# Layer 1's queries and keys projected densely and moved into padded strips by DMA, the first group's squares on ScalarE, and groups of 3, 4, 5 and 4 sequences

## The chip, the cores and the metric

The kernel runs on one core of one Trainium2 chip. The metric is the device time of one execution in microseconds (us). The kernel before took 1684.3 us, the median of three runs (1683.4, 1684.3, 1684.37).

## What is computed

Sixteen sequences of 512 tokens with 128 features pass through two transformer layers, all in float32. With LN for the normalization of a token's features without weights:

```
n  = LN(x)
x1 = x + linear_attention(n) + mixture_of_experts(n)          # layer 0
n1 = LN(x1)
y  = x1 + softmax_attention(n1) + channel_mix(n1)             # layer 1
```

Both attentions have 16 heads of 8 features. The linear attention of layer 0 uses rotated queries and keys and a running sum. The mixture has 8 experts with 512 hidden features (`square(relu(h @ w_fc)) @ w_proj`); a router picks two for every token and weighs them, and a shared expert of the same form works on all tokens. Layer 1's attention lets the queries of a chunk of 64 tokens see all keys up to the end of their chunk; its probabilities are scaled by a factor that is computed from their row sum, then normalized again. The channel mix blends each token with the one before it, and computes `sigmoid(r) * (square(relu(k)) @ W_v)`.

Layer 1's score needs q and k alone:

```
qkv    = n1 @ W_qkv.T                     # (16, 512, 384), in heads of 8
scores = einsum('bhtd,bhsd->bhts', q_c, k_c) * 8 ** -0.5
```

## The kernel before

**An order that is planned.** The program isn't emitted as it is written. A recording layer (class `Program`, from line 225) takes every operation with the tiles that it reads and writes (`call`, line 247; `add`, line 289), and `run` (line 330) then emits them by a list schedule: each engine takes, of the operations whose inputs its cost table says are ready, the one that comes first in the recorded order. The costs stand in lines 213 to 216: a DMA on SP's queue has 80 ns of issue and, besides, a landing time from its bytes (line 273); a weight load of two DMAs has 300 ns. The resulting order on each engine is fixed in the program. SyncE (SP) issues all plain DMAs in this one order, so that a DMA whose wait isn't over holds up those behind it; GpSimd does the same with its squares and its indirect DMAs. Every operation is emitted by one helper, so that the profile gives line 259 for nearly all of them; the names of their tiles tell them apart.

**Groups.** Tokens are sent to their experts in groups of sequences, `GROUPS = (3, 4, 4, 3, 2)` (line 47). For each group, `dispatch` (line 1038) normalizes the sequences, routes their tokens, and writes them sorted by expert into rows in DRAM (an indirect DMA for each 128 tokens and each of the two experts, line 1091). Each expert's rows are padded to whole tiles of 128; a group of n sequences has `(2 * 4n * 128 + 8 * 127) // 128` slot tiles (`slot_count`, line 53): 23, 31, 39 and 47 for n = 2, 3, 4 and 5. `slot_tiles` (line 1122) runs over them four at a time: fetch rows `xg`, transpose them, load each tile's expert weights `wf` and `wp` (256 KB each, four buffers of each; lines 1146 and 1149), multiply, relu on ScalarE, square, multiply, and write `results` to DRAM. The square of a first pair runs on GpSimd, that of a second pair on VectorE, and in group 0 all on VectorE (line 1177).

**Layers.** `layer0` runs the linear attention and the shared expert of a group's sequences one by one; their x1 goes to DRAM. `layer1` takes the sequences of the group before. Its sequences overlap: `body(b)` (line 1529) weighs the values of sequence b, and in between its steps are those of `operands(b, 1)` and then of `head(b + 1)` (line 1510), which ends with `operands(b + 1, 0)`. `head` gathers the experts' results from DRAM (`combine`, line 1215: two times four indirect DMAs into a tile `back` with two buffers, each added to x1), normalizes, transposes into `xp`, and does the channel mix and the values.

**Operands of layer 1's attention** (`operands`, line 1294). A score matmul has 32 rows, four side by side in TensorE. The 16 heads are worked in pairs, eight heads as a half u (0 or 1), so that a half has four strips of 32 rows. A strip holds a pair's 16 features and, behind them, rows with constants: they hide the keys that a query may not see, and take the row maximum of each head. So that q and k land in strips, the projection's weights are padded: `wqk1` has 4 blocks of 128 columns, of which 64 are used. Each half takes two 128x512 matmuls (tile `qk`). VectorE adds constants on the way from PSUM: `qa` is the query part plus `aug_q`; `ka` has two versions, one for each head of the pair, each the key part times a 0/1 column (`parity`) plus `aug_k`. Then the scores (`sc`) are computed once for their row maxima (VectorE, tile `maxima`), the maxima are transposed (`mx`) and subtracted in `qa`, and `weighted` (line 1349) computes the transposed scores (`st`), their exponentials on ScalarE (`ex`) and the product with the values (`o`). `qa` and `ka` have two buffers each.

The functions that the change touches:

Of the kernel before, what the change touches and what calls it, by code (L numbers as in the profile page):

```python
# [45 lines left out]

GROUPS = (3, 4, 4, 3, 2)
FIRST = [sum(GROUPS[:g]) for g in range(len(GROUPS))]
# [4 lines left out]
def slot_count(gt):  # L53
# [31 lines left out]
    ("causal", P), ("rank", E), ("upper", P), ("ones", P), ("tile", SLOT_TILES),  # L85
    ("aug_q", T), ("aug_k", 2 * T), ("parity", 2),
)
# [70 lines left out]
class Base:  # L158


    def __init__(self, slots, make):
        self.slots, self.make, self.tile = slots, make, None
        self.writers, self.readers = [], []
        self.left, self.free_at, self.users = 0, 0.0, []
# [60 lines left out]
class Program:  # L225
# [21 lines left out]
    def call(self, name, api, method, args, kw):  # L247
        views = [a for a in (*args, *kw.values()) if isinstance(a, View)]
        o = kw.get("out", args[0] if args else None)
        writes = [o.base] if isinstance(o, View) else []  # L250
        reads = [v.base for v in views if v is not o]
        n = math.prod(o.shape[1:]) if isinstance(o, View) else 0
        later = 0.0

        def made(a):
            return a.made() if isinstance(a, View) else a

        def emit():
            return getattr(api, method)(*map(made, args), **{k: made(a) for k, a in kw.items()})  # L259

        if name == "PE":
            later = 60.0
            form = (args[1].shape[0], o.shape[0])
            if method == "transpose":
                cost = 112.0
            elif args[1].shape[0] == 32:
                cost = max(0.425 * n, 56.0)
            elif o.shape[0] == 32:
                cost = max(0.425 * n, 56.0)
            else:  # L270
                cost = max(1.68 * n, 224.0)
        elif method == "dma_start":
            cost, later = 80.0, 512.0 * n
        else:
            form = method if (name, method) in COSTS else None
            if name == "DVE" and method in ("tensor_scalar", "tensor_scalar_min", "tensor_scalar_max"):
                form = "fast"
            if method in ("tensor_reduce", "bn_stats"):
                n = math.prod(args[1].shape[1:])
            least, each = COSTS[name, form]  # L280
            cost = least + each * n
            if kw.get("func", args[2] if len(args) > 2 else None) == AF.Sqrt:
                cost += 2600.0
        op = self.add(name, emit, reads, writes, cost, later)
        if name == "PE":
            (self.unit_of[0] if self.unit_of else op).form = form
        return op

    def add(self, name, emit, reads, writes, cost, later=0.0):
# [11 lines left out]
        for base in writes:  # L301

            op.needs.update(o for o in base.writers if o.engine != "SP" or name != "SP")
            op.needs.update(base.readers)
        for base in reads:
            base.readers.append(op)
        for base in writes:
            if base.readers:
                base.writers, base.readers = [], []
            base.writers.append(op)  # L310
# [176 lines left out]
def two_layers(ctx: ExitStack, tc: tile.TileContext, x, small, const, w_fc, w_proj, out):  # L487
# [32 lines left out]

    const_sb = fixed.tile([P, _CONST_N], F32, tag="const", name="const_sb")
    small_sb = fixed.tile([P, _STAYS_N], F32, tag="small", name="small_sb")
# [14 lines left out]
    x_in = {b: load_x(b, "x_in", 2) for b in range(2)}  # L537
    lo = _CONST_AT["aug_q"][0]
    SP.dma_start(const_sb[:, 0:lo], const[:, 0:lo])
    raw = {}  # L540
# [5 lines left out]
    for names in (_STAYS[:2], _STAYS[2:]):  # L546
# [3 lines left out]
        SP.dma_start(small_sb[:, slo:shi], small[:, lo:hi])  # L550
    lo = _CONST_AT["aug_q"][0]
    SP.dma_start(const_sb[:, lo:], const[:, lo:])
    program.lag = 250
# [25 lines left out]
    sin = c_("sin").rearrange("p (t d) -> p t d", d=4)  # L579
    aug_k = c_("aug_k").rearrange("p (o t) -> p o t", o=2)  # L580

    program.lag = 200

    wqk1 = fixed.tile([P, 4, 4, 32], F32, tag="wqk1", name="wqk1")
    G.memset(wqk1, 0.0)
    given1 = raw["wqk1"].rearrange("p (su j o e) -> p su j o e", su=4, j=4, o=2)
    for o in range(2):
        V.tensor_copy(wqk1[:, :, :, o * DH : (o + 1) * DH], given1[:, :, :, o, 0:DH])

# [532 lines left out]
    def slot_tiles(g):  # L1122
# [41 lines left out]
        def hidden(xgT, ws, q, pair):  # L1164
# [11 lines left out]

            (V if pair or g == 0 else G).tensor_tensor(o, o, o, ALU.mult)
            return h
# [36 lines left out]
    def combine(x1, b):  # L1215
# [4 lines left out]
        for j in range(2):  # L1220
            y = p2.tile([P, NT, D], F32, tag="back", name=f"back_{b}_{j}", bufs=2)
            for t in range(NT):
# [70 lines left out]

    def operands(xT, b, u):

        ps = big(f"qk1_{b}_{u}")
        for i in range(2):
            M.matmul(
                ps[:, i, :], wqk1[:, 2 * i + u, :, :].rearrange("p j e -> p (j e)"), xT,
                start=True, stop=True,
            )
        qa = p2.tile([P, T], F32, tag="qa", name=f"qa_{b}_{u}")
        V.tensor_tensor(qa, ps[:, 0, :], c_("aug_q"), ALU.add)
        ka = p2.tile([P, 2, T], F32, tag="ka", name=f"ka_{b}_{u}")
        for o in range(2):  # L1310
            V.scalar_tensor_tensor(
                ka[:, o, :], ps[:, 1, :], c_("parity")[:, o : o + 1], aug_k[:, o, :],
                ALU.mult, ALU.add,
            )
        yield
# [25 lines left out]
        for t in range(NT):  # L1341
            M.transpose(
                pm[:, t * P : (t + 1) * P], mx[:, t, :, :].rearrange("p j e -> p (j e)"), ident
            )
        V.tensor_tensor(qa, qa, pm, ALU.subtract)
        yield
        return qa, ka

# [161 lines left out]
    def head(b):  # L1510
# [6 lines left out]
        yield from combine(x1, b)  # L1517
        xp = p2.tile([P, T + 1], F32, tag="xp", name=f"xp_{b}", bufs=2)
        G.memset(xp[:, 0:1], 0.0)
        yield from layernorm_T(x1, xp[:, 1 : T + 1], f"1_{b}", "xn1", 1)  # L1520
        yield
        base = yield from channel_mix(x1, xp, b)
        yield
        vp = values(xp[:, 1 : T + 1], b)
        yield
        qm, ka = yield from operands(xp[:, 1 : T + 1], b, 0)
        return xp, base, vp, qm, ka

    def body(b, state):


        xp, base, vp, qm, ka = state
        o0, (qm, ka) = yield from weighted(
            qm, ka, vp, b, 0, operands(xp[:, 1 : T + 1], b, 1), 2
        )
        o1, got = yield from weighted(qm, ka, vp, b, 1, head(b + 1), 3)
        behind1.append(tail([o0, o1], base, b))
        return got
# [61 lines left out]
def _constants():  # L1600
# [14 lines left out]
    aug_q, aug_k = np.zeros((4, 32, T), f), np.zeros((4, 32, 2, T), f)  # L1615
    parity = np.zeros((4, 32, 2), f)
    for o in range(2):
        aug_k[:, PAIR + o, o] = 1.0
        parity[:, o * DH : (o + 1) * DH, o] = 1.0
    for t in range(NT):  # L1620
        aug_q[:, PAIR + 2 + t, t * P : t * P + P // 2] = HIDDEN
        aug_k[:, PAIR + 2 + t, :, t * P + P // 2 : (t + 1) * P] = 1.0
    c["aug_q"], c["aug_k"] = aug_q.reshape(P, T), aug_k.reshape(P, 2 * T)
    c["parity"] = parity.reshape(P, 2)
    inv = (f(10000.0) ** (-np.arange(4, dtype=f) / f(4))).astype(f)
# [65 lines left out]
```

## Time and profile before

| | |
|---|---|
| median of the runs | 1684.3 us |
| profiled execution, its own time | 1683.1 us |
| its span in the trace | 1681.3 us |
| TensorE matmul (PE) busy | 1566.0 us, 93% |
| VectorE (DVE) busy | 1220.5 us, 73% |
| ScalarE (ACT) busy | 763.4 us, 45% |
| GpSimd (POOL) busy | 405.0 us, 24% |
| mean granted TensorE clock | 0.973 |
| mean transfer | 100 GB/s |

All durations below come from the one profiled execution. A group's row reads: line, engine, operation, output and input tiles with their shapes, count; then busy time in us and mean ns of one; then the idle time of the engine just before them, and what ended it. PEld is the weight load that overlaps the matmuls. A float32 matmul has two records in the trace, so that counts of matmuls are twice those of the code; a transpose has one. In the slices, each digit is a fortieth of the span, in tenths of busy time (9 is 90% or more), and PEclk the clock that was granted to TensorE.

### The profile page before, as it was taken

The page shows a single profiled execution, that of the slowest core. Times are in us where ns is not written, and L with a number is a line of the kernel's source. Part 1 is how long each engine was busy: PE and PEld are TensorE (multiplying, and loading weights), DVE is VectorE, ACT ScalarE, POOL GpSimd, SP SyncE. Part 2 cuts the span into 40 slices and gives each one's busy share as a digit, 9 for nine tenths or more (in the row PEclk, how much of TensorE's full clock was granted, in tenths as well). Part 3 has the DMA queues.
Part 4 walks back from the last instruction along what each step waited for, and adds up shares of the span by engine and source line. Part 5 has one row for each costly group of instructions (what it writes and reads, how often), then busy time and mean ns, then how long its engine had stood idle before and what let it go on. Part 6 is the DMA issues. An engine that isn't in the chain of part 4 may idle for free.

```text
span 1681.3 us, 36447 instructions
## 1 busy us (share of the span) xinstructions
PE 1566.0 (93%) x14503; PEld 1027.3 (61%) x14503; DVE 1220.5 (73%) x2520; ACT 763.4 (45%) x1175; POOL 405.0 (24%) x389
## 2 busy tenths in 40 slices
PE   5898889999999999999999999999999999999996
PEld 3687766576756566665766656656665566555443
DVE  7876269767479875977678884968587867676773
ACT  3343334535445554445445553453545543534434
POOL 2404362162115211251014321140115010104000
PEclk8899999999999999999999999999999999999888
DMA  5377857143433532332332332313133223011000
GB/s 173 110 219 223 247 185 218 47 136 98 125 96 94 162 93 69 116 95 75 95 98 81 103 95 79 103 60 114 49 93 89 63 72 101 8 44 29 19 1 13
DMA packets 155129, 167.78 MB, mean 100 GB/s; under 512 B 13264, under 2 KB 100688, under 8 KB 154960
## 3 DMA queue, kind: packets, MB, share of 16 engines
q1 hardware_dynamic: 146768, 148.67, 29.7%
q0 software_dynamic: 8192, 16.79, 3.2%
q8 instruction: 114, 1.87, 0.4%
q14 instruction: 55, 0.45, 0.1%
HBM read 123.59 MB, written 41.81 MB: 98 GB/s over the span
## 4 chain that ended last, share of the span: by engine, by line
PE 55%; DVE 13%; ACT 3%; issue 1%; ACTq 0%; DVEq 0%
PE sc L259 11%; PE o L259 10%; PE st L259 8%; PE yg_ps L259 5%; DVE maxima L259 4%; PE hg_ps L259 4%; PE y L259 4%; PE qk L259 3%; PE h_ps L259 2%; ACT ex L259 1%; PE ho_a L259 1%; PE qkv L259 1%; PE oh_a L259 1%; PE mx L259 1%; PE cm_r L259 1%
## 5 line engine op out<-in xcount | busy, mean ns | idle before, releaser
L259 DVE TENSOR_REDUCE maxima<-sc 128x2 f32<-128x768 f32 (+2 forms) x448 | 385.4, 913 | 74.4 <-PE sc L259 71.4
L259 ACT ACTIVATE ex<-st 128x1024 f32<-128x1024 f32 x320 | 312.4, 1025 | 183.2 <-PE st L259 174.0
L259 PE MATMUL sc<-ka,qa 32*128 32x512 f32 (+2 forms) x1792 | 214.5, 518 | 7.5 <-DVE maxima L259 3.9
L259 PE MATMUL st<-qa,ka 32*128 32x384 f32 (+3 forms) x2048 | 209.3, 467 | 9.3 <-ACT ex L259 4.6
L259 DVE TENSOR_TENSOR am<-sc,const_sb 128x1024 f32<-128x1024 f32 x128 | 151.3, 1217 | 81.5 <-PE sc L259 76.6
L259 PE MATMUL yg_ps<-wp,hg 128*128 128x128 f32 x1304 | 182.1, 283 | 18.4 <-DVE hg L259 6.3
L259 PEld LDWEIGHTS yg_ps<-wp,hg 128*128 128x128 f32 x1304 | 160.0, 192 | 61.3 <-issue 32.1
L1091 POOL DMA_INDIRECT rows<-xn,pl_slot x128 | 131.4, 1026 | 224.0 <-DVE pl_slot L259 46.8
L259 PE MATMUL hg_ps<-xgT,wf 128*128 128x128 f32 x1304 | 176.1, 280 | 9.0 <-DMA wf<-in_w_fc 3.6
L1110 POOL DMA_INDIRECT back<-results,pl_slot x128 | 127.2, 994 | 220.2 <-PE st L259 45.6
L259 PEld LDWEIGHTS hg_ps<-xgT,wf 128*128 128x128 f32 x1304 | 158.7, 193 | 32.9 <-issue 13.4
L259 PE MATMUL o<-ex,vpad 128*32 128x512 f32 (+3 forms) x2048 | 175.7, 445 | 1.1 <-ACT oT_a L259 0.6
L259 PEld LDWEIGHTS st<-qa,ka 32*128 32x128 f32 x2048 | 103.6, 185 | 78.1 <-issue 27.0
L259 ACT ACTIVATE hg<-hg_ps 128x1024 f32<-128x1024 f32 x84 | 84.0, 1000 | 137.0 <-PE hg_ps L259 123.0
L259 PEld LDWEIGHTS sc<-ka,qa 32*128 32x128 f32 x1792 | 90.5, 188 | 69.0 <-issue 21.4
L259 POOL TENSOR_TENSOR hg<-hg 128x1024 f32<-128x1024 f32 x34 | 65.1, 1914 | 276.4 <-ACT hg L259 276.1
L259 PEld LDWEIGHTS o<-ex,vpad 128*32 128x32 f32 x2048 | 52.5, 109 | 88.0 <-issue 66.0
L259 DVE TENSOR_TENSOR hg<-hg 128x1024 f32<-128x1024 f32 (+1 forms) x50 | 58.4, 1168 | 59.3 <-ACT hg L259 45.7
L259 ACT COPY oTs<-o 128x256 f32<-128x256 f32 (+1 forms) x96 | 42.6, 444 | 125.4 <-PE o L259 113.6
L259 PE MATMUL sc<-q0m,k0T 32*128 32x256 f32 x1024 | 82.1, 412 | 3.3 <-ACT ex L259 1.4
L259 ACT COPY yg<-yg_ps 128x256 f32<-128x256 f32 x84 | 31.0, 369 | 112.5 <-PE yg_ps L259 77.0
L259 PE MATMUL o<-am,vpad 128*32 128x128 f32 x2048 | 77.0, 277 | 1.2 <-DVE am L259 0.9
(189 smaller groups left out, 2216.8 us busy)
## 6 DMA issues: line engine op xcount, KB each, us to landing
wf<-in_w_fc SPq DMA_DIRECT2D x163, 256.0 KB
wp<-in_w_proj SPq DMA_DIRECT2D x163, 256.0 KB
results<-yg SPq DMA_DIRECT2D x79, 128.0 KB
xg<-rows SPq DMA_DIRECT2D x37, 256.0 KB
rows<-zeros SPq DMA_DIRECT2D x2, 2496.0 KB
x_in<-in_x SPq DMA_DIRECT2D x16, 256.0 KB
x<-x SPq DMA_DIRECT2D x16, 256.0 KB
out<-rr SPq DMA_DIRECT2D x16, 256.0 KB
```

What stands on the lines that cost most here:

```text
L259: return getattr(api, method)(*map(made, args), **{k: made(a) for k, a in kw.items()})
L1091: i = nc.gpsimd.indirect_dma_start(out=rows.made()[:, :], out_offset=bass.IndirectOffsetOnAxis(ap=slot.made(), axis=0), in_=row.made(), in ...
L1110: "POOL", lambda: nc.gpsimd.indirect_dma_start(out=o.made(), out_offset=None, in_=results.made()[:, :], in_offset=bass.IndirectOffsetOnAxi ...
```

## The change

It has three parts, and what they need around them.

- **q and k without padding.** `wqk1` becomes 2 blocks of 128 columns. A new function `dense`, called in `head` ahead of the channel mix, multiplies once for q and once for k, for both halves; ScalarE copies them to SBUF. The strips `qa` and `ka` are made once for each half, and filled with the constants by DMA. `operands` then moves q and k of a half into them by 12 DMAs on SP's queue (4 of 16 rows for `qa`, 8 of 8 rows for `ka`; a row has 2 KB). As `qa` has to keep its constants, the subtraction of the maxima writes a new tile `qm`.
- **Squares of group 0** run on ScalarE, behind their relu.
- **Groups** are 3, 4, 5 and 4 sequences. The normalized tiles of a group then need five buffers instead of four; `back` and `xp` have one buffer instead of two.

Small changes in the recording layer: a DMA's bytes are counted from its rows, and a tile that is written in parts after it was read keeps the order to the earlier readers and writers for each part.

```diff
-GROUPS = (3, 4, 4, 3, 2)
+GROUPS = (3, 4, 5, 4)
...
-            cost, later = 80.0, 512.0 * n
+            cost, later = 80.0, 4.0 * n * (o.shape[0] if isinstance(o, View) else P)
...
+            op.needs.update(base.before)
...
             if base.readers:
+                base.before = base.writers + base.readers
                 base.writers, base.readers = [], []
...
-    wqk1 = fixed.tile([P, 4, 4, 32], F32, tag="wqk1", name="wqk1")
-    G.memset(wqk1, 0.0)
-    given1 = raw["wqk1"].rearrange("p (su j o e) -> p su j o e", su=4, j=4, o=2)
-    for o in range(2):
-        V.tensor_copy(wqk1[:, :, :, o * DH : (o + 1) * DH], given1[:, :, :, o, 0:DH])
+    wqk1 = fixed.tile([P, 2, P], F32, tag="wqk1", name="wqk1")
+    given1 = raw["wqk1"].rearrange("p (h e) -> p h e", e=32)
+    V.tensor_copy(
+        wqk1.rearrange("p s (h e) -> p (s h) e", e=DH), given1[:, :, 0:DH]
+    )
...
-            (V if pair or g == 0 else G).tensor_tensor(o, o, o, ALU.mult)
+            if g == 0:
+                S.activation(o, o, AF.Square)
+            else:
+                (V if pair else G).tensor_tensor(o, o, o, ALU.mult)
...
-            y = p2.tile([P, NT, D], F32, tag="back", name=f"back_{b}_{j}", bufs=2)
+            y = p2.tile([P, NT, D], F32, tag="back", name=f"back_{b}_{j}", bufs=1)
...
+    strips = []
+
+    def make_strips():
+        for u in range(2):
+            qa = p2.tile([P, T], F32, tag="qa", name=f"qa_{u}")
+            ka = p2.tile([P, 2, T], F32, tag="ka", name=f"ka_{u}")
+            (lo, hi), (klo, khi) = _CONST_AT["aug_q"], _CONST_AT["aug_k"]
+            first = [
+                SP.dma_start(qa, const[:, lo:hi]),
+                SP.dma_start(ka.rearrange("p o t -> p (o t)"), const[:, klo:khi]),
+            ]
+            strips.append((qa, ka, first))
+
+    def dense(xT, b):
+
+        if not strips:
+            make_strips()
+        ps = big(f"qk1_{b}")
         for i in range(2):
-            M.matmul(
-                ps[:, i, :], wqk1[:, 2 * i + u, :, :].rearrange("p j e -> p (j e)"), xT,
-                start=True, stop=True,
-            )
-        qa = p2.tile([P, T], F32, tag="qa", name=f"qa_{b}_{u}")
-        V.tensor_tensor(qa, ps[:, 0, :], c_("aug_q"), ALU.add)
-        ka = p2.tile([P, 2, T], F32, tag="ka", name=f"ka_{b}_{u}")
-        for o in range(2):
-            V.scalar_tensor_tensor(
-                ka[:, o, :], ps[:, 1, :], c_("parity")[:, o : o + 1], aug_k[:, o, :],
-                ALU.mult, ALU.add,
-            )
+            M.matmul(ps[:, i, :], wqk1[:, i, :], xT, start=True, stop=True)
+        q = p2.tile([P, T], F32, tag="xn1", name=f"q1_{b}", bufs=1)
+        k = p2.tile([P, T], F32, tag="k1", name=f"k1_{b}", bufs=1)
+        S.copy(q, ps[:, 0, :])
+        S.copy(k, ps[:, 1, :])
+        return q, k
+
+    def operands(qk, b, u):
+        q, k = qk
+        qa, ka, first = strips[u]
+        for j in range(4):
+            at, r = u * P // 2 + j * PAIR, 32 * j
+            rows = [SP.dma_start(qa[r : r + PAIR, :], q[at : at + PAIR, :])]
+            for o in range(2):
+                rows.append(SP.dma_start(
+                    ka[r + o * DH : r + (o + 1) * DH, o, :], k[at + o * DH : at + (o + 1) * DH, :]
+                ))
+            for i in rows if first else ():
+                after(i, first)
+        strips[u] = (qa, ka, [])
         yield
...
-        V.tensor_tensor(qa, qa, pm, ALU.subtract)
-        yield
-        return qa, ka
+        qm = p2.tile([P, T], F32, tag="qm", name=f"qm_{b}_{u}")
+        V.tensor_tensor(qm, qa, pm, ALU.subtract)
+        yield
+        return qm, ka
...
-        xp = p2.tile([P, T + 1], F32, tag="xp", name=f"xp_{b}", bufs=2)
+        xp = p2.tile([P, T + 1], F32, tag="xp", name=f"xp_{b}", bufs=1)
...
+        qk = dense(xp[:, 1 : T + 1], b)
+        yield
         base = yield from channel_mix(x1, xp, b)
...
-        qm, ka = yield from operands(xp[:, 1 : T + 1], b, 0)
-        return xp, base, vp, qm, ka
+        qm, ka = yield from operands(qk, b, 0)
+        return qk, base, vp, qm, ka
```

## Prediction

> **What bounds the kernel now.** I read the page first: the span, the busy times, the slices.
>
> ```profile
> span 1681.3 us, 36447 instructions
> PE 1566.0 (93%) x14503; PEld 1027.3 (61%) x14503; DVE 1220.5 (73%) x2520; ACT 763.4 (45%) x1175; POOL 405.0 (24%) x389
> PE   5898889999999999999999999999999999999996
> DVE  7876269767479875977678884968587867676773
> PEclk8899999999999999999999999999999999999888
> ```
>
> TensorE is the bound: nine tenths from the eighth slice to the last but one, VectorE beside it mostly at 6 to 9 tenths. So an edit that takes TensorE work away should pay almost in full, and one that only relieves another engine little. Two things limit that. In the first 336 us TensorE idles 54 us (busy times of that stretch), where layer 0 runs almost alone. And a busy TensorE isn't one at its peak, as TensorE's timeline near the end shows (start, duration, engine, operation, count, idle before):
>
> ```profile
> 1614.00 1.15 PE L259 MATMUL sc<-ka,qa 32*128 32x384 f32 x16
> ...
> 1617.81 4.65 PE L259 MATMUL sc<-ka,qa 32*128 32x384 f32 x20 [0.28 <-DVE maxima L259]
> ```
>
> Sixteen score matmuls take 1.15 us, then twenty take 4.65, since VectorE's maxima free their PSUM. The stretches around it (busy times of PE, PEld, DVE, ACT, POOL; clock; DMA):
>
> ```profile
> 1550.00:1560.00 10.00, 8.22 (x41) 3.34 (x41) 9.33 (x16) 0.21 (x1) 0.00 (x0) 0.68 0.00 0
> ...
> 1620.00:1630.00 10.00, 9.09 (x30) 3.75 (x32) 8.59 (x16) 1.37 (x2) 0.00 (x0) 0.50 0.01 2
> ...
> 1640.00:1650.00 10.00, 9.67 (x106) 5.95 (x108) 7.01 (x10) 4.83 (x6) 0.00 (x0) 1.00 0.10 29
> ```
>
> 30 matmuls "busy" for 9.09 us at clock 0.50 against 106 in 9.67 us at 1.00: with only layer 1 left, VectorE bounds the score phases.
>
> **The change part by part.** First what TensorE and VectorE lose, from the groups (busy, mean ns of one):
>
> ```profile
> L259 PE MATMUL qk<-xp,wqk 128*128 128x512 f32 x128 | 63.5, 600 | 0.1
> L259 PE MATMUL yg_ps<-wp,hg 128*128 128x128 f32 x1304 | 182.1, 283 | 18.4 <-DVE hg L259 6.3 <-ACT xgT L259 4.0 <-issue 2.3
> L259 PE MATMUL hg_ps<-xgT,wf 128*128 128x128 f32 x1304 | 176.1, 280 | 9.0 <-DMA wf<-in_w_fc 3.6 <-DVE maxima L259 3.0 <-ACT xgT L259 2.0
> L259 PE MATMUL xgT_ps<-const_sb,xg 128*128 128x128 f32 x163 | 29.0, 287 | 2.1 <-DVE sums L259 1.4 <-ACT hg L259 0.5 <-DVE state L259 0.2
> L259 DVE SCALAR_TENSOR_TENSOR ka<-qk,const_sb 128x512 f32<-128x512 f32 x64 | 45.6, 742 | 0.0
> L259 DVE TENSOR_TENSOR qa<-qk,const_sb 128x512 f32<-128x512 f32 x32 | 22.0, 689 | 21.6 <-PE qk L259 21.4
> ```
>
> q and k take two matmuls a sequence instead of four: half of 63.5 = 31.8 us off TensorE. Slot tiles are 31+39+39+31+23 = 163 before and 31+39+47+39 = 156 after; seven fewer are 56 of 1304 records in two groups, 7.8 + 7.6 us, and 7/163 of 29.0 = 1.2. Together 48.4 us on the bounding engine: **-48.4**.
>
> VectorE loses the ka and qa rows, 67.6 us, and some 16 squares of 1.2 us. ScalarE gains 32 copies (the like row, xp from ln_ps 128x512, has 595 ns: 19 us) and 16 squares at 1.0 (15.6 us): 763 becomes about 798 us, 47% of the span, so it stays hidden. The first group's squares ran where VectorE has room (11.28 us busy of the 42 from 168 to 210 us, its DMA share 0.83); the square now follows its relu on one engine, 2.0 us, about what relu, handover and 1.2 us took. Bounds -4 to +3, I take 0.
>
> What VectorE's relief is worth isn't in any idle row, but in stretched matmuls. At the dense pace one half's scores are three units of 1.14 and two of 1.15 us, 5.7, so 183 us for 32 halves against 214.5 shown; the same sum for st gives 184 against 209.3. 56 us are stretch. The six operations removed per sequence stood between projection and scores. Bounds 0 to 30; I take a sixth, **-10**, since the 24 us of maxima per sequence stay.
>
> **The strips.** 12 small DMAs now carry q and k of each half into place: 384 on SP's queue. None of the kind is in the trace; the nearest rows are SP's own neighbours:
>
> ```profile
> 424.96 0.33 SPq L1149 DMA_DIRECT2D wp<-in_w_proj  x1
> 425.39 0.38 SPq L259 DMA_DIRECT2D results<-yg  x1
> ```
> ```profile
> 500.21 0.33 SPq L259 DMA_DIRECT2D x<-xs  x1
> 502.26 0.39 SPq L259 DMA_DIRECT2D xs<-in_x  x1
> ```
>
> Back to back 0.43 us apart; and a load that had to wait for a store came 2.05 us after it, which is issue and landing. So 12 take 12 x 0.43 + 2.05 = 7.2 us, and 16 (as often stand together) 8.9. The Trainium skill speaks against this edit: *DMA: Bandwidth & Descriptors*, Rules for kernel authors, says to coalesce many small transfers, as under 64 KB one pays mostly overhead; these have 16 and 32 KB. If overhead were paid one after another, 12 x 2.05 = 25 us per half, 787 us in all, could not hide. By the rows only issue is serial: 7.2. I follow the rows, since the 2 us of several transfers run beside each other.
>
> What covers 7 to 9 us is TensorE's order. Counting the instructions between the q,k projection and a first half's first scores in the changed program, at the mean of their rows: 4.9 us for sequence 0, 9.3 and 9.4 for 12 and 7, 13 to 43 for the others. The second half's k may only go once the previous sequence has read its strip; from that to the scores stand 7 to 42 us, against 8 x 0.43 + 2.05 = 5.5. Sequence 0 so waits 4 us, the others hardly. **+6** (0 to 25). Behind a batch on SP wait weights, gathered rows, x loads: the planner counts 0.08 us for a DMA, 0.43 is real, so weights come 5.6 us later than planned. At 0.43 each, after most batches some 4 us are left between issue and the matmul, after four under 3: **+4** (0 to 20).
>
> The gather buffer goes from two to one: the second gather of a sequence waits for four accumulations (0.35 us each) on GpSimd's queue, and behind it GpSimd's squares (1.9 us) and rr steps, for which TensorE's expert matmuls can wait. Heads run half a sequence ahead; exposed it would be 16 x 5 us. **+2** (0 to 15). One buffer for xp and the new k tile: their readers end early, nothing.
>
> **The end.** In the old program 1.8 sequences of probabilities stand behind the last layer-0 matmul (it ends at 1574.8 us, 106.5 before the end); in the new order 4.0. So 2.2 more sequences run with no layer-0 work to fill. By the rows layer 1 needs 51.6 us of TensorE a sequence (sc 13.4, st 13.1, o 11.0, qk 4.0, the rest 10.1), 49.6 after the change. The pace with no filler is in the last results' additions (VectorE's timeline):
>
> ```profile
> 1583.01 0.68 DVE L259 TENSOR_TENSOR rr<-rr,y 128x512 f32<-128x512 f32 x1
> ...
> 1644.95 0.68 DVE L259 TENSOR_TENSOR rr<-rr,y 128x512 f32<-128x512 f32 x1
> ```
>
> 62 us. But the last head then waited for layer 0 (its x1 is stored at 1577.5, its scores begin at 1607), so weighting and scores did not overlap; that is gone when layer 0 ends earlier. VectorE's need in layer 1, by its rows, drops from 47 to 43 us a sequence. I take 54 a sequence: 2.2 x 4.4 = **+10** (0 at TensorE's pace; 27 at 62). Here too a rule bears: *TensorE: Matmul & The Clock Gate*, HAM oscillation, says an idle gap over about 3.4 us halves the clock. The trace's 0.50 and 0.68 came with gaps of 1.2 us at most, but sparse matmuls; by the rule my tail would keep its clock, by the row a score phase loses it. The 54 includes some of that.
>
> Sum: -48.4 - 10 + 6 + 4 + 2 + 10 = -36.4. Against the profiled execution's 1683.1 us (span 1681.3 and 1.8 around it) that is 1646.7; the median of the runs lies 1.2 higher: **1648**.
>
> **The rivals.** *The tail keeps the old pace, nothing relaxes:* -48.4 + 6 + 4 + 2 + 27 = -9.4, 1675. For it: VectorE near TensorE in need, 43 to 49.6. Against: the late head was its cause.
> *VectorE was the hidden bound:* strips free, stretch -20, tail +3: -65, 1619. For: 56 us of stretch. Against: the maxima remain.
> *SP's queue becomes the bound (slower):* a batch waits behind a weight load whose buffer isn't free, or weights behind a batch, and TensorE's fixed order stands still. Without SP's costs the sum is -46.4; over 32 halves it turns at 46.4 / 32 = 1.45 us each. At 2 us it is +17.6, 1702. For: SP waits 356.7 us for yg_ps before loading wp. Against: in the order, what precedes each batch on SP is released 10 us or more of TensorE work before its scores.
>
> **Chances.** Forecast (1636 to 1660) 0.52; old tail pace 0.16; hidden bound 0.14; SP slower 0.12; within 0.2%, which is about what a measurement here can tell from no change, 0.06. So faster 0.82, same 0.06, slower 0.12. The range 1620 to 1678 leaves out slower, same and a little below.
>
> **What would show it.** qk with 64 records near 32 us; yg_ps and hg_ps with 1248; VectorE near 1130 us busy; idle before sc put down to DMA qa or ka some 6 us in all, most at sequence 0; idle before hg_ps for wf up by a few us; last layer-0 matmul about 220 us before the end, results 50 to 56 us apart there, sc mean below 518 ns. I am wrong if sc waits for strips in most sequences, if SP's issue of one strip is far above 0.43 us, or if the results of the last three come 60 us apart.

## The result and the profile after

The changed kernel took 1699.6 us (median of six runs, 1696.5 to 1711.2) against 1684.3 us of the kernel before in the same job: 1.0105 times as long, 95% interval 1.0071 to 1.0139. The forecast was 1648 us, 52 us lower. The changed kernel's profiled execution took 1711.2 us, with a span of 1709.4; it is the slowest of the six, 11.5 us over their median, and its differences to before are read with that in mind.

The page's first lines, as they were shown of before (busy us, share, instructions; then tenths in 40 slices):

```profile
span 1709.4 us, 36600 instructions
PE 1581.6 (93%) x14316; PEld 1028.8 (60%) x14316; DVE 1121.8 (66%) x2348; ACT 785.4 (46%) x1208; POOL 396.1 (23%) x386
PE   5899889999889989999999999999999999999996
DVE  6863157838457766596674968476765777767863
PEclk8899998999999999999999999999999999989997
```

VectorE lost 99 us of work (the forecast has some 87), and TensorE 187 matmul records (183 by the code's count); yet TensorE is busy for 15.6 us longer. The groups show that the work itself went (busy, mean ns; idle before, and for what):

```profile
L260 PE MATMUL qk<-xp,wqk 128*128 128x512 f32 x64 | 31.2, 604 | 1.5 <-issue 0.7 <-ACT xp L260 0.7
L260 PE MATMUL yg_ps<-wp,hg 128*128 128x128 f32 x1248 | 174.9, 284 | 10.5 <-ACT hg L260 3.0 <-POOL hg L260 2.6 <-ACT yg L260 2.4
L260 PE MATMUL hg_ps<-xgT,wf 128*128 128x128 f32 x1248 | 174.9, 285 | 26.0 <-DMA wf<-in_w_fc 22.1 <-DVE maxima L260 1.6 <-ACT xgT L260 1.1
L260 PE MATMUL sc<-ka,qa 32*128 32x512 f32 (+2 forms) x1792 | 238.6, 530 | 7.6 <-DMA ka<-k 3.1 <-ACT ex L260 1.1 <-DVE am L260 1.0
```

qk is halved, to 31.2 us. But the same 1792 records of sc are busy for 238.6 us instead of 214.5, and ahead of hg_ps TensorE idles 22.1 us for the weights wf, where it was 3.6. The tile `wf` isn't touched by the change. What it waits for is on SyncE's queue (start, duration, DMA, count; the duration of several is from the first's start to the last's end):

```profile
444.80 0.38 SPq L260 DMA_DIRECT2D xg<-rows  x1
458.07 5.00 SPq L260 DMA_DIRECT2D qa<-q  x8
463.17 6.09 SPq L260 DMA_DIRECT2D ka<-k  x8
470.58 0.37 SPq L1145 DMA_DIRECT2D wf<-in_w_fc  x1
```

and on ScalarE and TensorE at that time:

```profile
457.46 0.59 ACT L260 COPY q<-qk 128x512 f32<-128x512 f32 x1 [3.79 <-DVE o0n L260]
463.15 1.15 PE L260 MATMUL sc<-q0m,k0T 32*128 32x256 f32 x16
473.52 2.05 PE L260 MATMUL hg_ps<-xgT,wf 128*128 128x128 f32 x8 [9.23 <-DMA wf<-in_w_fc]
```

SyncE stands 13 us at the first strip, until ScalarE has copied q; then 16 strips go out one by one in 11.2 us, 0.6 to 0.8 us each; only then comes the weight load that TensorE's next matmul needs. TensorE stands for 9.2 us. From the start of one strip to the start of the next these are 0.63 us (`qa`, 5.00 / 8) and 0.76 (`ka`, 6.09 / 8). The prediction counted 0.43 for this, and the planner that fixes the order counts 0.08. (The duration of a single strip, without the pause to the next, is 0.580 us for `qa` and 0.625 for `ka` in the median of the execution.)

The stretched scores show the other side of this. In the first sequence (TensorE's timeline, then the busy times of PE, PEld, DVE, ACT and POOL in the stretch, its clock, DMA share and GB/s):

```profile
251.84 6.21 PE L260 MATMUL sc<-ka,qa 32*128 32x512 f32 x8 [1.90 <-DMA ka<-k]
260.84 2.09 PE L260 MATMUL sc<-ka,qa 32*128 32x512 f32 x8
252.00:258.00 6.00, 6.00 (x9) 1.74 (x9) 1.23 (x1) 0.00 (x0) 0.00 (x0) 0.50 0.12 24
```

Eight score matmuls take 1.14 us elsewhere; these are "busy" for 6.21 us, while SyncE issues the `ka` strips that they read. Two things are in that. The clock is 0.50, and at this clock the next eight take 2.09 us, so about 1 us is the clock's. The other 4 us come from matmuls that start one after another instead of four side by side, which fits strips that arrive one by one. A wait for strips thus appears partly as idle time (1.90 us) and partly as busy time.

The end went as forecast in this kernel. The last layer-0 matmul ends 230.4 us before the end of the span (forecast some 220), and the last results are 53 to 56 us apart (forecast 50 to 56):

```profile
1508.69 0.69 DVE L260 TENSOR_TENSOR rr<-rr,y 128x512 f32<-128x512 f32 x1 [0.92 <-PE y L260]
1564.03 0.68 DVE L260 TENSOR_TENSOR rr<-rr,y 128x512 f32<-128x512 f32 x1
1617.07 0.68 DVE L260 TENSOR_TENSOR rr<-rr,y 128x512 f32<-128x512 f32 x1
1672.87 0.69 DVE L260 TENSOR_TENSOR rr<-rr,y 128x512 f32<-128x512 f32 x1
```

So the loss lies ahead of that, where both layers run: layer 0 ends at 1479 us, where the forecast has some 1425.

### The profile page after: what moved, and what is told of

Same layout as the page of the kernel before. It is cut to its first block, busy times and chain, and to the rows that moved or that the text cites. A ratio compares the mean times of both kernels' runs of the same rounds, so it can differ in the third digit from the quotient of the medians.

```text
span 1709.4 us, 36600 instructions
## 1 busy us (share of the span) xinstructions
PE 1581.6 (93%) x14316; PEld 1028.8 (60%) x14316; DVE 1121.8 (66%) x2348; ACT 785.4 (46%) x1208; POOL 396.1 (23%) x386
## 4 chain that ended last, share of the span: by engine, by line
PE 69%; DVE 15%; ACT 5%; issue 4%; DMA 3%; SPq 3%; POOL 0%; ACTq 0%; DVEq 0%; POOLq 0%
PE sc L260 14%; PE o L260 13%; PE st L260 8%; PE yg_ps L260 7%; PE hg_ps L260 7%; PE y L260 5%; DVE maxima L260 5%; SPq L260 2%; PE qkv L260 2%; PE h_ps L260 2%; DMA wf<-in_w_fc 1%; PE qk L260 1%; PE ho_a L260 1%; ACT ex L260 1%; PE ln_ps L260 1%
## 5 line engine op out<-in xcount | busy, mean ns | idle before, releaser
L260 PE MATMUL sc<-ka,qa 32*128 32x512 f32 (+2 forms) x1792 | 238.6, 530 | 7.6 <-DMA ka<-k 3.1
L260 PE MATMUL st<-qm,ka 32*128 32x512 f32 (+3 forms) x2048 | 219.4, 474 | 14.2 <-DVE maxima L260 6.4
L260 PE MATMUL hg_ps<-xgT,wf 128*128 128x128 f32 x1248 | 174.9, 285 | 26.0 <-DMA wf<-in_w_fc 22.1
L260 PE MATMUL yg_ps<-wp,hg 128*128 128x128 f32 x1248 | 174.9, 284 | 10.5 <-ACT hg L260 3.0
L260 PEld LDWEIGHTS yg_ps<-wp,hg 128*128 128x128 f32 x1248 | 154.8, 194 | 45.4 <-issue 27.0
L260 PE MATMUL o<-ex,vpad 128*32 128x512 f32 (+3 forms) x2048 | 181.4, 456 | 0.5 <-ACT ex L260 0.3
L1090 POOL DMA_INDIRECT rows<-xn,pl_slot x128 | 126.3, 987 | 208.1 <-DVE pl_slot L260 38.6
L260 PEld LDWEIGHTS st<-qm,ka 32*128 32x128 f32 x2048 | 106.7, 188 | 90.7 <-issue 25.5
L260 PEld LDWEIGHTS sc<-ka,qa 32*128 32x128 f32 x1792 | 98.8, 192 | 91.5 <-issue 28.8
L260 POOL TENSOR_TENSOR hg<-hg 128x1024 f32<-128x1024 f32 x32 | 60.9, 1902 | 235.7 <-ACT hg L260 235.3
L260 DVE TENSOR_TENSOR hg<-hg 128x1024 f32<-128x1024 f32 (+1 forms) x32 | 38.0, 1187 | 58.9 <-ACT hg L260 58.4
```

What stands on the lines that cost most here:

```text
L1090: i = nc.gpsimd.indirect_dma_start(out=rows.made()[:, :], out_offset=bass.IndirectOffsetOnAxis(ap=slot.made(), axis=0), in_=row.made(), in ...
```

## The experiments

Each was timed in five rounds beside the kernel before, whose median was 1682.2 to 1686.7 us in the six jobs. First theory, **the plan**: the strips are cheap enough, but the planner counts 80 ns for a DMA that takes SyncE 500 to 760, and writes the strips into SyncE's queue ahead of weights that are due. Rivals: **the groups** (the long end costs more than +10), **the single buffers** of `back` and `xp`, **the squares**, and **SyncE itself** (the strips' issue is too much for one queue, however it is planned).

**Groups taken back, and groups alone.** The changed kernel with the five old groups; and the kernel before with the four new groups, with the single buffers that they came with.

```diff
-GROUPS = (3, 4, 5, 4)
+GROUPS = (3, 4, 4, 3, 2)
```

> The changed kernel with the groups of before (3, 4, 4, 3, 2); strips and squares as changed. Theory A (SyncE's one queue: strip DMAs of 0.5 to 0.7 us each, waiting for q and k, hold back the weight loads behind them): the cost stays with the strips, and the seven slot tiles come back, so 1700 to 1720 us. Theory B (the longer stretch of layer 1 alone at the end is what costs): with the old groups it goes away, 1655 to 1675 us. Theory C (the new order is just unlucky): anything, with no wait of its own that stands out.

> The kernel before with groups of 3, 4, 5 and 4 (and one buffer each for back and xp, which make room for the fifth normalized tile); q and k padded, no strips. Theory A: groups alone gain or lose little, the 15 us of seven tiles against some 10 us at the end, 1670 to 1690 us. Theory B: slower, 1700 us or more.

Measured: 1766.2 us with the old groups (1.0495, 1.0474 to 1.0516), and 1702.4 us for groups and single buffers alone (1.0104, 1.0082 to 1.0126). Both are slower than before, and the strips are far worse without the new groups. (The first kernel still has the single buffers and the squares of the change.) The waits of TensorE in the first of the two kernels (total us, times, longest):

```profile
PE hg_ps L260 <- DMA wf<-in_w_fc: 17.4, 10, 4.4
PE sc L260 <- DMA ka<-k: 16.4, 10, 5.0
```

**The plan told of the strips.** The changed kernel, the planner's cost alone changed; no operation is added or removed, only their order moves.

```diff
-            cost, later = 80.0, ...
+            part = isinstance(o, View) and o.shape[0] < P
+            cost, later = 640.0 if part else 80.0, ...
```

> The changed kernel, with the planner told 640 ns instead of 80 for a strip DMA, as measured on SyncE's queue (0.51 to 0.76 us). The work is the same. Theory A, in the form that the plan and the queue disagree: the weights and scores are put where they can be had, 1660 to 1680 us. Theory A, in the form that the queue's time itself is short: 1690 to 1700 us. Theory B: 1695 to 1705 us, no change.

Measured: 1670.1 us (0.9922, 0.9904 to 0.9940), 29.5 below the changed kernel and 13 below the kernel before. SyncE's queue at about the same place of the program:

```profile
444.94 0.58 SPq L260 DMA_DIRECT2D qa<-q  x1
445.61 1.41 SPq L260 DMA_DIRECT2D ka<-k  x2
448.33 0.36 SPq L1146 DMA_DIRECT2D wf<-in_w_fc  x1
448.95 0.35 SPq L1149 DMA_DIRECT2D wp<-in_w_proj  x1
449.35 1.47 SPq L260 DMA_DIRECT2D qa<-q  x1
451.59 0.35 SPq L1146 DMA_DIRECT2D wf<-in_w_fc  x1
```

The strips take as long as before, but weights go between them; TensorE's wait for wf falls from 22.1 to 4.8 us, and sc from 238.6 to 228.0:

```profile
PE hg_ps L260 <- DMA wf<-in_w_fc: 4.8, 6, 1.9
```

Idle time is the smaller part of the gain. From the changed kernel's profiled execution to this one the span falls by 36.1 us (1709.4 to 1673.3), TensorE's idle time by 9.5 and its busy time by 26.6, for the same matmuls. The mean granted clock rises from 0.953 to 0.963. An estimate of what the lower clock costs is the span times one minus the clock: 80 us and 62 us (too high for both, since it counts idle time too). So up to about half of the 36 us is matmuls at a lower clock, and not waiting itself.

**The strips on another queue.** The changed kernel with the 12 DMAs of a half issued by GpSimd (the planner counts 80 ns for them there too).

```diff
-            rows = [SP.dma_start(qa[r : r + PAIR, :], q[at : at + PAIR, :])]
+            rows = [G.dma_start(qa[r : r + PAIR, :], q[at : at + PAIR, :])]
...
-                rows.append(SP.dma_start(
+                rows.append(G.dma_start(
```

> The changed kernel with the 384 strip DMAs issued from GpSimd's queue instead of SyncE's; all else as changed. Theory A: the weights no longer stand behind strips, the waits of expert matmuls for wf fall from 22 us to below 5, and the time to 1655 to 1680 us, unless GpSimd's own queue (squares, gathers) becomes the block. Theory B: no change, 1695 to 1705 us.

Measured: 1714.7 us (1.0192, 1.0168 to 1.0215). The wait for wf falls to 1.8 us, so it was the strips that held the weights. But GpSimd is now busy for 592 us instead of 396, and what it does else comes late:

```profile
PE cm_v L260 <- POOL xk L260: 21.1, 5, 6.9
```

The wait has moved, not gone.

**The single buffers alone, and the squares alone.** The kernel before with one buffer each for `back` and `xp`; and the changed kernel with the first group's squares on VectorE again.

```diff
-            if g == 0:
-                S.activation(o, o, AF.Square)
-            else:
-                (V if pair else G).tensor_tensor(o, o, o, ALU.mult)
+            (V if pair or g == 0 else G).tensor_tensor(o, o, o, ALU.mult)
```

> The kernel before, only with one buffer each for back and xp instead of two. Groups alone, with these two buffers, took 1702 us. If the single buffers cost it, this takes 1695 to 1705 us too; if the groups cost it (a longer end with layer 1 alone), this stays at 1680 to 1690 us.

> The changed kernel with the first group's squares back on VectorE. My sum put this part at 0 (-4 to +3): 1696 to 1703 us. If the squares on ScalarE cost, below 1694; if they help, above 1705.

Measured: 1708.9 us for the buffers (1.0148, 1.0124 to 1.0171), 25 us where the forecast had 2. And 1701.1 us with the squares back (1.0124, 1.0095 to 1.0154): no difference to the changed kernel's 1.0105, as forecast. Set beside the buffers alone, the groups of e2 gain 0.44 of a per cent, 7.4 us, where the forecast had 16.6 less 10. The two intervals touch, and the runs below show that another order of the groups alone moves the time by more than this, so that the agreement may be chance.

**The plan with the old groups, and with all of SyncE's costs.** e1 with the strips planned at 640 ns; and the changed kernel with 640 ns for a strip, 430 for any other DMA of SyncE, and 1150 instead of 300 for a pair of weights. The diff shows the second of the two.

```diff
-            cost, later = 80.0, ...
+            part = isinstance(o, View) and o.shape[0] < P
+            cost, later = 640.0 if part else 430.0, ...
...
-            program.add("SP", emit, [expert.base], [wf.base, wp.base], 300.0, ...
+            program.add("SP", emit, [expert.base], [wf.base, wp.base], 1150.0, ...
```

> The changed kernel with the planner at 640 ns for a strip DMA and the groups of before. With 80 ns the old groups took 1766 us, 66 more than the new ones. If that was the plan's mistake at the strips, it falls far more than the 30 us that the new groups gained, to 1675 to 1700 us; if the old groups themselves don't go with the strips, it stays at 1730 or more.

> The changed kernel with the planner at measured costs for the whole of SyncE's queue: 640 ns for a strip DMA, 430 for any other, 1150 for a pair of weight loads (300 before). If the plan's disagreement with the queue is what costs, it is at or below the 1670 us of 640 ns alone, 1655 to 1672; if only the strips' disagreement counts, 1668 to 1675; if the gain at 640 ns was luck of one order among many, anything from 1665 to 1710.

Measured: 1697.4 us (1.0082, 1.0058 to 1.0105), 69 below e1; and 1666.6 us (0.9893, 0.9867 to 0.9919), the time of the changed kernel less 33. Beyond the strips' price the other two costs bring 3.5 us, which the intervals (0.9867 to 0.9919 against 0.9904 to 0.9940) don't separate.

**Which buffer.** The kernel before with one buffer for `back` alone (`bufs=1` on line 1221), and for `xp` alone (line 1518).

> The kernel before with one change: the tile that the routed rows of a sequence are fetched into (back) has one buffer, not two; xp keeps two. Both single buffers together cost 25 us (1708.9 against 1683.5). Theory A, the fetches carry the cost (the second fetch of a sequence cannot start until VectorE has added the first, and GpSimd's queue, in which it waits, holds everything behind it): 1698 to 1709. Theory B, xp carries it (GpSimd's memset of the next xp waits in the queue until the copies and the adds that read the last one are done): within 5 us of the kernel before, 1679 to 1689. If both are needed, something like 1690.

> The kernel before with one change: xp, the shifted k of layer 1, has one buffer, not two; back keeps two. Theory A, the fetches carry the 25 us: within 5 us of the kernel before, 1679 to 1689. Theory B, xp carries it: 1698 to 1709, with GpSimd waiting for VectorE's xk ahead of the memset of xp some tens of us longer in sum than before.

Measured: 1703.3 us for `back` (1.0110, 1.0095 to 1.0125), 1684.7 for `xp` (0.9994, 0.9984 to 1.0004). Most of the 25 us is `back` (1.1 of 1.48 per cent, some 19 us), and nothing measurable is `xp`. GpSimd's timeline with one `back`:

```profile
751.09 0.96 POOL L1091 DMA_INDIRECT rows<-xn,pl_slot  x1 [0.30 <-issue]
754.24 0.98 POOL L1110 DMA_INDIRECT back<-results,pl_slot  x1 [2.19 <-PE o L259]
755.52 0.96 POOL L1110 DMA_INDIRECT back<-results,pl_slot  x1 [0.30 <-PE o L259]
758.96 0.94 POOL L1110 DMA_INDIRECT back<-results,pl_slot  x1 [2.49 <-PE hg_ps L259]
759.93 1.05 POOL L259 TENSOR_TENSOR xk<-xk 128x512 f32<-128x512 f32 x1
```

The second half's four fetches of a sequence (the last comes at 761.14) stand here behind a group's scatters (`rows`, from 702.6 us on). With two buffers, in the kernel before, they had gone out ahead of them, at 588.2 to 593.8 us, and xk's square and the next sequence's `xp` came earlier:

```profile
593.83 0.94 POOL L1110 DMA_INDIRECT back<-results,pl_slot  x1 [1.07 <-PE hg_ps L259]
745.66 1.05 POOL L259 TENSOR_TENSOR xk<-xk 128x512 f32<-128x512 f32 x1
783.93 0.10 POOL L259 MEMSET xp<- 128x1 f32 x1 [1.71 <-PE qk L259]
```

With one buffer that `xp` begins at 793.3 us.

**Does the buffer explain the changed kernel?** The changed kernel, and e8, with two buffers for `back`. The room comes from two routing tiles that share the space of two dead ones:

```diff
-            a = tiny.tile(shape, dtype, tag=f"pl_{tag}", ...
+            shared = {"both": "rt_p2", "pos": "rt_pr"}.get(tag, f"pl_{tag}")
+            a = tiny.tile(shape, dtype, tag=shared, ...
...
-            y = p2.tile([P, NT, D], F32, tag="back", name=f"back_{b}_{j}", bufs=1)
+            y = p2.tile([P, NT, D], F32, tag="back", name=f"back_{b}_{j}", bufs=2)
```

> The changed kernel with back at two buffers again; to make room, two tiles of the routing arithmetic (both and pos) share the space of two that are dead by then. Theory A, the single back buffer costs the changed kernel about what it costs the kernel before (19 us alone, 1703.3 against 1686.5): 1678 to 1688, layer 1's seventh to eleventh sequences 8 to 17 us earlier. Theory B, behind the wrongly planned strips the single buffer is hidden, and the strips alone explain the loss: 1695 to 1704.

> The kernel with the measured costs for SyncE's queue in the planner (1666.6 us) and back at two buffers. If the two causes add: 1644 to 1655, at the blind forecast of 1648. If the single buffer costs nothing once the order is right: 1662 to 1670, and some 18 us of the forecast stay unexplained.

Measured: 1702.6 us (1.0110, 1.0086 to 1.0134) and 1665.9 us (0.9886, 0.9865 to 0.9907). Neither moved. My theory that the two causes add fell: what one buffer costs depends on the order in which it is tried. In the order of before, the fetches have scatters to get ahead of; why the other order doesn't suffer isn't shown.

**Is a right plan good for any kernel?** The kernel before, which has no strips, with e8's other costs (430 and 1150).

> The kernel before with only the planner's costs for SyncE's queue set to measured ones (430 ns for a DMA, 1150 ns for a pair of weights); it has no strips. Theory A, the gain of 30 us from such costs is that of the strips: 1678 to 1688, no change. Theory B, the costs help any kernel with this planner, strips or none: 1655 to 1675.

Measured: 1694.5 us (1.0053, 1.0033 to 1.0073). It loses 9 us. So the 30 us aren't the gift of better costs in general. But it is neither theory's number: a new order by itself moves the time by several us.

**The rest of the gap.** Even planned, 1666.6 is 18.6 above the forecast. Three kernels, all with e8's costs: groups of 3, 5, 5 and 3 (one sequence less at the end); the five old groups with two buffers each, so that only the q and k part and the squares remain of the change; and groups of 3, 5, 4 and 4 as a control.

> The changed kernel with measured costs for SyncE's queue in the planner (1666.6 us), and groups of 3, 5, 5 and 3 instead of 3, 4, 5 and 4: the same 156 slot tiles, but one sequence fewer of layer 1 left without layer-0 work at the end (that end takes 229 us of 1668 there). Theory A, a sequence at the end costs 56 us against the 40 or so that its matmuls need among dense work, so the prediction's tail term (4.4 us a sequence) was three times too small: 1647 to 1657. Theory B, the tail term was right: 1659 to 1666.

> The changed kernel with measured costs for SyncE's queue, but the five old groups and two buffers each for back and xp, as before: what is left of the change is layer 1's q and k without padding, and the squares on ScalarE. Theory A, the four groups lose as much at the end as they save in padding, and the q and k part brings what the prediction gave it (32 on TensorE, up to 10 of stretch): 1645 to 1655. Theory B, the four groups gain some 5 us: 1668 to 1678. Theory C, the strips' issue on SyncE eats most of the q and k part even when it is planned for: 1675 to 1685.

> A control for the order: groups of 3, 5, 4 and 4, with measured costs; the same slot tiles and the same end as the kernel of 1666.6 us, only the sizes of the second and third group exchanged. Both theories of the tail: 1661 to 1672. A larger difference would say that the order of the groups by itself moves the time by as much as the tail is said to.

Measured: 1684.7 us (1.0003, 0.9980 to 1.0025), 1673.9 us (0.9924, 0.9899 to 0.9949), 1683.7 us (0.9977, 0.9958 to 0.9996). The control spoils the first comparison: exchanging two groups alone costs 17 us against e8 (14 by the ratios to the kernel before), and against that control the shorter end gains nothing. Whether the end was priced right can't be told from these. Against the kernel before, the q and k part in e15 gains 0.76 of a per cent, about 12 us, where its terms in the forecast (−31.8 − 10 + 6 + 4) sum to −31.8. But e15 also has the two costs that by themselves made the kernel before slower (e13, 1.0053). Against e13, whose planner has the same costs, e15 gains 1.3 per cent, some 22 us. Which of the two is the fair comparison can't be told where an order alone moves the time so far; both fall short of 31.8. What e15's trace shows at the end (windows from the last layer-0 matmul to the end: PE, PEld, DVE, ACT, POOL busy, clock, DMA share, GB/s), e15 first, before second:

```profile
1545.40:1670.70 125.30, 104.09 (x790) 48.54 (x790) 71.30 (x160) 51.63 (x66) 2.92 (x3) 0.84 0.06 16
```

```profile
1574.80:1681.30 106.50, 86.41 (x726) 42.54 (x726) 62.55 (x138) 46.58 (x59) 2.92 (x3) 0.87 0.04 13
```

Up to the last layer-0 matmul the program is 29.4 us faster, nearly all of the 31.8 taken from TensorE. But layer 1 hasn't come further by then: 790 matmul records are left, not 726, and the end takes 18.8 us longer. (By the same estimate as above, 0.16 of 125.3 us against 0.13 of 106.5, the lower clock accounts for at most 6 of these.) And its pace is the old one:

```profile
1571.66 0.68 DVE L260 TENSOR_TENSOR rr<-rr,y 128x512 f32<-128x512 f32 x1
1634.40 0.68 DVE L260 TENSOR_TENSOR rr<-rr,y 128x512 f32<-128x512 f32 x1
```

It is 62.7 us between results, against 61.9 before, though VectorE no longer makes qa and ka; and these two results come 11.4 and 10.6 us earlier than their like in the kernel before (1583.01 and 1644.95), not 29.4. The mean of sc is 522 ns (518 before) and of st 468 (467), so the stretch didn't shrink:

```profile
L260 PE MATMUL sc<-ka,qa 32*128 32x512 f32 (+2 forms) x1792 | 217.1, 522 | 5.6 <-DVE maxima L260 2.1 <-ACT ex L260 1.6 <-DVE am L260 0.8
L260 PE MATMUL st<-qm,ka 32*128 32x384 f32 (+3 forms) x2048 | 211.1, 468 | 8.4 <-DVE maxima L260 4.1 <-ACT q0m L260 1.1 <-DVE am L260 1.1
```

The end of e8, the changed kernel with all costs, isn't at the forecast's pace either:

```profile
1515.18 0.69 DVE L260 TENSOR_TENSOR rr<-rr,y 128x512 f32<-128x512 f32 x1
1582.19 0.69 DVE L260 TENSOR_TENSOR rr<-rr,y 128x512 f32<-128x512 f32 x1 [4.74 <-PE y L260]
1631.17 0.69 DVE L260 TENSOR_TENSOR rr<-rr,y 128x512 f32<-128x512 f32 x1
```

The results come 67.0 and 49.0 us apart, 59 in the mean of three with the one before (1454.17), where the forecast has 54 and the changed kernel itself some 55. Put into the prediction's own term, 2.2 x (59 - 49.6) is 21 us instead of 10, an estimate; no run separates it.

**Was the plan's 33 us luck?** Since an order alone can move 17 us, the comparison was repeated with the other two arrangements: the changed kernel, 80 ns a strip as it is, with groups of 3, 5, 4, 4 and of 3, 5, 5, 3.

> The changed kernel as it is (the planner counts 80 ns for a strip), with groups of 3, 5, 4 and 4. With measured costs the same groups took 1683.7 us. Theory A, a wrong plan for the strips costs any arrangement of the groups some 30 us or more (33 with 3, 4, 5, 4): 1705 to 1730, TensorE waiting for wf and ka some 20 us. Theory B, the 33 us were the luck of one order: 1675 to 1695.

> The changed kernel as it is (80 ns for a strip), with groups of 3, 5, 5 and 3; with measured costs these took 1684.7 us. Theory A: 1705 to 1730. Theory B: 1675 to 1695.

Measured: 1750.6 us (1.0392, 1.0377 to 1.0407) and 1747.9 us (1.0355, 1.0331 to 1.0379). In a table:

| groups | strips planned at 80 ns | at 640 ns | difference |
|---|---|---|---|
| 3, 4, 5, 4 | 1699.6 | 1670.1 (e3), 1666.6 (e8) | 29 to 33 |
| 3, 4, 4, 3, 2 | 1766.2 (e1) | 1697.4 (e7) | 69 |
| 3, 5, 4, 4 | 1750.6 (e17) | 1683.7 (e16, all costs) | 67 |
| 3, 5, 5, 3 | 1747.9 (e18) | 1684.7 (e14, all costs) | 63 |

Four of four lose 29 us or more; exchanging groups under a right plan had moved 17. The changed kernel's own arrangement is the one that loses least. In e17 TensorE waits 16.0 us for wf, 8.0 for ka and 7.4 for gathered rows; in e16, its like, 2.7, nothing listed, and 4.0. The clock differs here too, 0.950 against 0.963: by the estimate above up to 25 of the 61 us between the two spans, in the pair e1 and e7 up to 36 of 62, and in e18 and e14 up to 32 of 69.

## Why the prediction was wrong

**The step that failed** is the weights "behind a batch": "+4 (0 to 20)", with "+6 (0 to 25)" for the strips themselves. The prediction saw that "the planner counts 0.08 us for a DMA, 0.43 is real", and priced it by counting, in the changed order, how much TensorE work stands between issue and need. Two things were wrong in it. One strip follows another after 0.63 to 0.76 us in the batch shown, not after 0.43: the neighbours taken as the nearest rows were whole-tile transfers, not strips of 8 and 16 rows. And the work was counted as if every batch started on time: SyncE also waits, at the head of a batch, for a copy of q or k, and all weights behind it inherit that. In the profile after (SyncE's waits, total us, times, longest):

```profile
SPq L260 <- ACT k L260: 120.2, 13, 24.1
```

No run separates the two. Together they cost the 30 to 33 us that a right plan gives back, against 10 in the sum; planned, e15 shows no listed wait for ka and 4.5 us for wf, 0.9 more than before. A term for the clock was missing as well: by the estimates above, up to about half of the loss is matmuls at a lower clock, and the sum priced waits alone. The slower rival, "SP's queue becomes the bound", had this place and gave 1702 (that this is so near is luck: its 2 us for each half were assumed); the argument against it looked only at what the scores wait for, not at the weights that stand behind the strips. Its name was wrong in one point: SyncE isn't too slow for the strips, since the same DMAs on the same queue gain 13 us when they are planned.

**VectorE's relief (−10)** didn't come: e15's sc and st have the old means, and the end its old pace. VectorE lost 85 us there, and the stretch of TensorE's matmuls stayed. The prediction's own reserve, that the maxima stay, is the likely reason; no run tests it.

**TensorE's 48.4 us** went nearly as counted (qk 63.5 to 31.2, yg_ps 182.1 to 174.9 for 7 tiles less; hg_ps only 176.1 to 174.9, where 7.6 were forecast), but 48.4 us of work were not 48.4 us of time. In e15 the work taken away shortened the part where layer 0 fills the gaps, and the end grew by 18.8 us: layer 1 hadn't come along. The reading that fits is that this work was filler for layer 1 as well. The prediction priced the end only for the groups (2.2 sequences), at +10, and not for the q and k part. This reading rests on one trace and its control before. With orders that differ by 14 to 17 us for no visible reason, the 10 to 20 us that the q and k part fell short show up at the end, but their cause isn't shown.

**The buffers (+2)**: in the old order 25, mostly from `back`; in the changed one nothing measurable (e11, e12). The number held; whether for the reason given ("heads run half a sequence ahead") isn't shown.

**The end (+10)**: its length (220 forecast, 230 measured) and its pace (54, measured 53 to 56) were right for the changed kernel. Once the plan is right, the pace is 59 (e8), so that this agreement is in part luck, and up to 11 us of the gap may lie here. The groups' gain, −6.6 forecast and −7.4 measured between e5 and e2, agrees, but is smaller than what an order alone moves. **The squares (0)**: right.

Together: 1648, plus 20 for the q and k part (−12 in e15 for −31.8), less 3 for groups and buffers (−7 from e15 to e8 for −4.6), is e8's 1666; plus 33 for the plan it is the measured 1699.6. These steps are differences between runs, and would add up whatever their causes; taken from e13, the q and k part is short by 10 only, and the other 10 go to the order that e8's costs make. The fastest kernel of the study is the changed one with measured costs for SyncE's queue in the planner: 1666.6 us, and 1665.9 with two buffers for `back`, 1.1% below the kernel before.

## What to carry to other kernels

Where a planner fixes the order, a new kind of operation needs its own measured cost in the plan before the kernel is judged: here the same operations in another order were 30 to 69 us apart, more than the change itself was worth. For a queue that issues in order, ask of every new entry not only who waits for it, but what stands behind it and for what it waits itself. Where such a wait stops the bounding engine, its clock belongs in the price, and not its idle time alone. And work taken from the bounding engine need not pay in full: in e15 the end grew by 18.8 of the 29.4 us that the part ahead of it lost.

## What the runs showed of the hardware

A DMA's price on SyncE isn't one number. A strip from SBUF to SBUF took 0.507 us at least for 16 rows of 2 KB (`qa`) and 0.624 for 8 rows (`ka`), with single ones up to 1.7; most whole-tile stores, loads and weight loads beside them took 0.33 to 0.39 in the median. On GpSimd's queue the same strips took 0.487 and 0.515 us in the median (e4). So here the smaller transfer is the dearer one for the queue that issues it, of 8 rows against 16 and of strips against whole tiles; for the second, the whole tiles also go to or from DRAM, and no run separates the two.

And a long wait is paid a second time in the clock. After the 9.23 us in which TensorE stood, its clock was halved (busy us of PE, PEld, DVE, ACT, POOL; granted clock; DMA share, GB/s):

```profile
473.50:477.00 3.50, 3.48 (x10) 2.20 (x10) 0.00 (x0) 0.00 (x0) 0.00 (x0) 0.50 0.86 262
477.00:480.00 3.00, 3.00 (x33) 2.19 (x32) 0.00 (x0) 1.19 (x2) 1.04 (x1) 0.96 0.02 5
```

For 3.5 us the clock is 0.50: eight matmuls of hg_ps take 2.05 us, and 1.16 at 478 us. This is what the Trainium skill, *TensorE: Matmul & The Clock Gate*, HAM oscillation, says of gaps over some 3.4 us; here it added about 1.7 us to a wait of 9.2 (0.9 on hg_ps, 0.8 on the two cm_k that follow, which take 1.92 us against 1.12 in the trace of before). A gap of this length isn't needed, however: the clock of 0.50 at 252 us, shown further up, came behind gaps of at most 1.9 us in the ten us ahead of it, with few matmuls between them.
